# Experts' weights in four DRAM copies, constants of the start moved, and new limits for the planner of a hybrid block

## The chip, the cores and the metric

The kernel runs on one core of a Trainium2 chip, in one launch. Its time is device microseconds, the median of several runs. The core's engines have instruction queues of their own: TensorE (PE; its weight loads are shown apart as PEld), VectorE (DVE), ScalarE (ACT), GpSimd (POOL), and SyncE (SP), on which this kernel issues every DMA.

## The reference

The input x has 8 sequences of 512 rows of 128 numbers, all fp32. Four layers are applied one after another, each on the layernorm of x and each added to x:

```python
x = x + attn_a(layernorm(x))      # state-space layer ("mamba")
x = x + ffn(layernorm(x))         # 8 experts, all of them computed
x = x + attn_b(layernorm(x))      # attention, 16 heads of 8, window of 25 rows back and chunks of 10
x = x + ffn(layernorm(x))         # the same weights again
```

The state-space layer projects x by W_in, runs a convolution of three taps and a SiLU over both halves of the channels, and from one half forms delta, decay, B and C; it then scans over the 512 rows with 8 states in each of 64 channels:

```python
state = decay * state + (1 - decay) * tanh(b) * xb
y = sum(state * tanh(c)) + D * xb
out = concat([y, zb]) @ W_out.T
```

The expert layer weighs all eight experts by the product of two softmaxes:

```python
router_probs = softmax(x @ w_router)
gate_weights = softmax((x @ w_gating) / 0.1)
g = einsum("bsh,ehf->ebsf", x, w_gate)
u = einsum("bsh,ehf->ebsf", x, w_up)
expert_out = einsum("ebsf,efh->ebsh", silu(g) * u, w_down)
cw = router_probs * gate_weights
cw = cw / (sum(cw) + 1e-9)
out = einsum("ebsh,bse->bsh", expert_out, cw)
```

## The kernel before

**The main stream.** Nearly all of TensorE's time goes to the experts' products. `ffn_stream` goes through both expert layers (k = 0, 1), the 8 sequences b, the 8 experts e and four blocks of 128 hidden columns f. For each it issues `g` and `u` (128 hidden columns by 512 rows) and `y` (back to 128 columns, summed over f in one PSUM bank). To keep fp32 precision, every product is three matmuls of split operands: each weight is a rounded part and a rest ("low", `wg`, `wu`, `wd`; the rests are made by the lane `lows` on GpSimd in the beginning), and so are the activations `xt` and `h`. ScalarE takes the SiLU of `g`, VectorE multiplies by `u`, and the hidden block `h` is split into its parts by a cast (ScalarE or VectorE) and a subtraction on GpSimd.

**The experts' weights.** `ffn_prep` computes for a sequence the layernorm, the transposed `xt`, the router's logits, the softmaxes and `cw`. `cw` is transposed (`cps`, copied to `cwt`) and written to DRAM (`cwd`). The lane `spreads` reads it back for each expert as `cwb`, 128 partitions by 512 rows, all partitions alike. VectorE multiplies `y` by `cwb` in place, and GpSimd adds the result to `acc`. There are two buffers for `cwb`.

**The order.** The order of instructions on each engine is not written by hand. While the program is built, a planner issues them one by one: `Engine.__getattr__` issues each instruction (so nearly all of them carry its line, L269, in the profile) and adds its estimated cost to a `Clock` with one time for each engine. Side work is written as generators ("lanes"), which yield the engine that they need next, or a condition. `Lanes.start` says when a lane's next step can begin by these estimates; a step on TensorE is let in between main products only if its operands are there by a margin, `SIDE`, and a larger one where the main stream would first have to be left for it: `JOIN`, or `JOIN_MAX`, `JOIN_ATT`, `JOIN_END` for certain lanes. `HELD` cuts how far ahead of its start a side step may be issued while the main stream waits; `LATE` and `PREP_DUE` set by when the router's exponentials and the preparation of a sequence are due, in sequences. Where the planner sees TensorE waiting, `keep_warm` puts a matmul on constants in (`warm` before the first expert, `idle` after it), if the gap is above `WARM_GAP`. ScalarE has to load a table when it goes from SiLU or tanh to exponentials and back.

**The start.** The first sequence is done in two halves of 256 rows, so that the experts begin early: `first_halves` does its state-space layer (convolution `mv`; `mxb`, `mzb`; `mbc`, `mde`, `macc`; `mbx`, `mcx`, `mdec`; the scan `mst`; the output `mo`) and `ffn_prep` its preparation. The first `SPLIT` experts of the first sequence are then computed for each half by itself, in products of 256 columns; the rest in products of 512. Constants are made meanwhile: `wxz`, the output weights scaled by D, in `mamba_consts` on ScalarE (two instructions, after the flag `done["halves"]`), and `route`, the router's weights with the gating part times 10, in `route_consts` on VectorE (two instructions, L1016 and L1018). The flag `done["quiet"]` holds back the lane `lows` and the second half's inputs while the first half's layernorm runs.

Of the kernel before, what the change touches and what calls it, by code (L numbers as in the profile page):

```python
# [18 lines left out]
P = 128  # L19
# [68 lines left out]

TABLES = {AF.Silu: (18,), AF.Exp: (0, 6), AF.Ln: (6,), AF.Tanh: (0, 18)}
INF = float("inf")  # L90
LAGS = {"T": 0.2, "A": 0.15, "V": 0.15, "P": 0.08}
TO_PE = 0.11
SAME = 0.125
AHEAD = 0.2
EDGE = 0.1
FIRST = 0.6
LATE = 0.3
SIDE = 0.5
JOIN = 2.0
JOIN_DUE = 0.0  # L100
JOIN_MAX = 6.0
JOIN_ATT = 3.0
JOIN_END = 2.0
MOST = 6
OTHERS = 4
AT_FIRST = 7
WARM = 3.5
WARM_GAP = 0.25
WARM_TO = 1.5
SECOND = 0.2  # L110
PRESS = 0.4
HELD = 0.18
MAMBA_DUE = 0.9
PREP_DUE = 0.9
ATT_LEAD = 2.5
EARLY = 5
SPLIT = 4
EARLIEST = 2 * (DEPTH + 1)


# [8 lines left out]
class Clock:  # L129
# [105 lines left out]
    def run(self, key, name, out, args, kw, after, wait):  # L235
        c = self.cost(key, name, out, args, kw)
        start = max(self.end[key] + wait, after, self.now if key == "T" else self.based(key))
        if key == "T":
            if start > self.end["T"] + 2.4:
                self.cold = start  # L240
            if start < self.cold + 3.4:
                c *= 2
        if key in "VP" and self.shares(key, name, out, args):
            start = self.with_port(start, c)
        self.end[key] = start + c
        if key == "S":
            start = max(start, self.now)
            row = out.shape[-1]
            rows = out.shape[0] * size(out) // row
            each = max(row * (2 if out.dtype == BF16 else 4), 512)  # L250
            move = rows * each / 200e3
            self.moved = max(self.moved, start + c + 0.8) + move
            return self.moved + 0.6 + move
        self.hop[key] = start + c
        return start + c + LAGS[key]

# [121 lines left out]
def block_kernel(ctx: ExitStack, tc: tile.TileContext, x, pack_a, pack_b, pack_c, w_qkv, mask, mask_t, w_o,  # L378
# [194 lines left out]
    def mamba_consts(sb, mc):  # L573
        table("natural_log_exp_and_others", 6)

        pick = sb.tile([P, L], F32, tag="dec", name="pick", bufs=5)[:, : 2 * DSTATE]
        pool.tensor_tensor(pick, ident[:, : 2 * DSTATE], ident[:, 32 : 32 + 2 * DSTATE], ALU.add)
        sel = sb.tile([P, 2 * NSTEP, 2, INNER], F32R, name="sel", bufs=1)
        for m in range(2):
            rows = pick[:, m * DSTATE : m * DSTATE + DSTATE].rearrange("p (s i) -> p i s", s=2)  # L580
            pool.tensor_copy(
                sel[:, m * NSTEP : m * NSTEP + NSTEP], rows[:, :, :, None].to_broadcast([P, NSTEP, 2, INNER])
            )
        mc["sel"] = sel.rearrange("p n s c -> p n (s c)")
        yield "A", pa_there

        nega = sb.tile([P, NSTEP], F32, name="nega", bufs=1)
        alog = pa[:, A_ALOG : A_ALOG + NSTEP]
        sp_ = sb.tile([P, NSTEP], F32, tag="sp_a", name="sp_a", bufs=1)
        act.activation(sp_, alog, AF.Abs)  # L590
        act.activation(sp_, sp_, AF.Exp, scale=-1.0)
        act.activation(sp_, sp_, AF.Ln, bias=1.0)
        win = [sb.tile([P, P], F32R, name=f"win_{i}", bufs=1) for i in range(2)]
        src = pa[:, A_WIN : A_WIN + P]
        act.copy(win[0], src)
        yield "V"
        dve.scalar_tensor_tensor(sp_, alog, 0.0, sp_, ALU.max, ALU.add)
        dve.tensor_scalar(nega, sp_, 1e-4, -1.0, ALU.add, ALU.mult)
        dve.tensor_tensor(win[1], src, win[0].bitcast(F32), ALU.subtract)
        mc["win"] = win  # L600
        yield "A"

        cap = sb.tile([P, NSTEP], F32, name="cap", bufs=1)
        act.activation(cap, nega, AF.Exp, scale=1e-4)
        table("silu_and_others", 18)

        yield "T", pc_there
        wp = yield from side([P, P], "wdt_ps")
        pe.matmul(wp, pc[:, 0:P], pc[:, P : 2 * P], start=True, stop=True)
        wdt = sb.tile([P, P], F32, name="wdt", bufs=1)  # L610
        yield "A"
        freed(act.copy(wdt, wp))
        mc["wdt"] = wdt

        wbc = sb.tile([P, P], F32, name="wbc", bufs=1)
        yield "P"
        for h in range(2):
            pool.tensor_copy(
                wbc[INNER * h : INNER * h + INNER].rearrange("p (c n) -> p c n", c=4),
                pa[:INNER, None, A_PBC : A_PBC + 32].to_broadcast([INNER, 4, 32]),  # L620
            )
        mc["wbc"] = wbc
        yield "V"
        dve.tensor_scalar(cap, cap, 1.0, None, ALU.min)
        mc["nega"], mc["cap"] = nega, cap

        yield lambda: "halves" in done
        yield "AV"
        wxz = sb.tile([P, P], F32, name="wxz", bufs=1)
        act.activation(wxz[:INNER], pa[:INNER, A_WOUT : A_WOUT + P], AF.Copy, scale=pa[:INNER, A_D : A_D + 1])  # L630
        mc["wxz"] = wxz, act.copy(wxz[INNER:], pa[INNER:, A_WOUT + P : A_WOUT + 2 * P])
        route_consts()
# [72 lines left out]
    def first_halves(sb, consts, h, xo):  # L705
# [12 lines left out]
        def half(c):  # L718
            cs = slice(c * HALF, c * HALF + HALF)
            v, xb = vs[c], xbs[c]  # L720
            yield "A"
            act.activation(v, h[:, cs], AF.Copy, scale=kc[1])
            yield "V"
            n = 1 - c
            dve.scalar_tensor_tensor(
                v[:, n:], h[:, cs.start + n - 1 : cs.stop - 1], kc[0], v[:, n:], ALU.mult, ALU.add
            )
            yield "V"
            e = dve.scalar_tensor_tensor(
                v[:, : HALF - c], h[:, cs.start + 1 : cs.stop + n], kc[2], v[:, : HALF - c], ALU.mult, ALU.add  # L730
            )
            if c:
                freed(e)
            yield "A"

            act.activation(xb[0:INNER], v[0:INNER], AF.Silu)
            there2 = act.activation(xb[INNER:P], v[0:INNER], AF.Silu)
            yield "T", there2
            pde, pbc = yield from sides(([P, HALF], f"mde0_{c}"), ([P, L], f"mbc0_{c}"))
            pbc = pbc[:, :HALF]  # L740
            pe.matmul(pbc, consts["wbc"][:INNER], xb[:INNER], start=True, stop=True)
            pe.matmul(pde, consts["wdt"][INNER:], xb[INNER:], start=True, stop=True)
            add[c](scanned(c, pbc, pde))

        def scanned(c, pbc, pde):
# [3 lines left out]
            def rows():  # L749
# [3 lines left out]
                act.activation(pbc[32:64], pbc[32:64], AF.Tanh)  # L753
                there["z"] = act.activation(zb, vs[c], AF.Silu)
                issued["tanh"] += 1
                yield "V"
                e = freed(dve.tensor_tensor(bc[32:64], pbc[32:64], bc[32:64].bitcast(F32), ALU.subtract))
                for m, into in enumerate((bxs, ccs)):
# [98 lines left out]
            for p in range(2):  # L857
                yield lambda: p in scans
                yield from undisturbed()
                yield "V", max(scans[p][1], ccs["t", p])  # L860
                cx = sb.tile([P, 2, HALF], F32, tag="acc", name=f"mcx0_{c}_{p}")
                e = freed(dve.tensor_tensor(cx, ccs[p], scans[p][0], ALU.mult))
                yield "T", e
                for t in range(2):
                    for i in range(2):
                        pe.matmul(
                            ops[t], cx[:, i, t * P : (t + 1) * P], pa[:, A_WOUT : A_WOUT + P],
                            start=False, stop=(p == i == 1),
                        )
            yield "V"  # L870
            part = xo[0][:, 2 * c : 2 * c + 2]
            for t in range(2):
# [150 lines left out]
    def ffn_prep(k, b, xc, t0=0, nt=NT):  # L1023
# [13 lines left out]
            done.pop("quiet", None)  # L1037
            done["calm"] = 0.0
        if t0 == 0:
            done["cw", k, b] = dram.tile([NT, NE, P], F32, tag="cwd", name=f"cwd_{nm}", bufs=3), 0.0, 0  # L1040
        cwd = done["cw", k, b][0]
        ready[k, b] = ready[k, b][0], cols.stop
        wr, = routes
# [28 lines left out]


        yield "V"
        cw = fp.tile([P, NT, NE], F32, tag="cw", name=f"cw_{nm}")[:, :nt]
        s4 = fp.tile([P, NT], F32, tag="s4", name=f"s4_{nm}")[:, :nt]
        z = fp.tile([P, NT], F32, tag="z", name=f"z_{nm}")[:, :nt]
        dve.tensor_reduce(s8, pr, AX.X, ALU.add)
# [11 lines left out]
        yield "T"  # L1090
        cps = yield from side([NT * NE, P], f"cps_{nm}")
        n = nt * NE
        pe.transpose(cps[:n], cw.rearrange("p t e -> p (t e)"), ident)
        yield "V"
        cwt = fp.tile([NT * NE, P], F32, tag="cwt", name=f"cwt_{nm}")
        freed(dve.tensor_copy(cwt[:n], cps[:n]))
        yield "S"
        e = sp.dma_start(out=cwd[t0 : t0 + nt].rearrange("t e p -> (t e) p"), in_=cwt[:n])
        done["cw", k, b] = cwd, e, cols.stop

    pos = [0.0]
# [21 lines left out]
    def ffn_stream():  # L1123
# [73 lines left out]
        def spreads():  # L1197

            for k in range(2):
                for b in range(B):  # L1200
                    todo = passes(k, b)
                    for i, (e, cs) in enumerate(todo):
# [6 lines left out]
                        n = cs.stop - cs.start  # L1209
                        cwb = fp.tile([P, L], F32, tag="cwb", name=f"cwb{k}_{b}_{e}_{cs.start}", bufs=2)[:, :n]  # L1210
                        state["cwb", (k, b, e, cs.start)] = cwb, sp.dma_start(
                            out=cwb.rearrange("p (t q) -> p t q", q=P),
                            in_=cwd[None, cs.start // P : cs.stop // P, e, :].to_broadcast([P, n // P, P]),
                        )

        def chunks(cs):
# [644 lines left out]
```

## Time and profile before

| | |
|---|---|
| median of 3 runs | 1353.25 us (1351.0 to 1355.0) |
| the profiled execution | 1351.62 us, span 1349.8 us |
| instructions on record | 29533 |
| DVE, ACT, POOL busy | 1036.8, 964.7 and 940.4 us |
| queue of the DMAs | 33.9% of 16 engines, 105.87 MB |
| `cwb` reads | 124 of 256 KB, 8 of 128 KB |
| mean granted TensorE clock | 0.996 |

The page describes one execution. A row of a group gives the line, the engine, the operation and its tiles (written tile <- read tiles, numbers left out), then counts and times. `PE u <- ACT h` among the waits means that a matmul into `u` waited until an instruction of ScalarE on `h` had ended; the numbers behind are the total in us, the times, and the longest. In a row of windows the numbers are: from and to, the length, the busy time of PE, PEld, DVE, ACT and POOL with instructions in brackets, the granted clock of TensorE as a share of full speed, the DMA engines' busy share and the GB/s moved.

### The profile page before, as it was taken

The numbers are of one execution on the slowest core, as the hardware profiler recorded it, in microseconds if no ns is written. First come the engines' busy times: TensorE is split into PE (matmuls) and PEld (weight loads), VectorE is DVE, ScalarE is ACT, GpSimd is POOL, SyncE is SP. The second block draws the span as 40 slices with busy tenths as digits, with TensorE's granted clock in tenths as the row PEclk, the third lists the DMA queues.
The fourth block names the chain that finished last, engine by engine and source line by source line (L and its number), as shares of the span: only waits on it lengthen the run. The fifth ranks groups of instructions, "written<-read, shape, count | busy, mean of one in ns | idle before, by whom it ended". The sixth has DMA issues, their size and how long they took to land.

```text
span 1349.8 us, 29533 instructions
## 1 busy us (share of the span) xinstructions
PE 1328.9 (98%) x10261; PEld 1053.3 (78%) x10261; DVE 1036.8 (77%) x3114; ACT 964.7 (71%) x1694; POOL 940.4 (70%) x1042
## 2 busy tenths in 40 slices
PE   7999999999999999999999999999999999999998
PEld 7877778788788877777777777777777777778887
DVE  6887888688888867898788887888888787855443
ACT  7768576867787556777777777777877767765654
POOL 5877576776767757666766767767677676777776
PEclk9999999999999999999999999999999999999999
DMA  3321304232112242344345444454544434222111
GB/s 126 95 72 38 87 24 101 62 81 73 45 48 56 63 85 54 73 97 118 79 103 111 99 106 100 104 109 89 118 91 104 119 71 88 61 69 55 40 40 40
DMA packets 230861, 107.75 MB, mean 80 GB/s; under 512 B 86417, under 2 KB 226616, under 8 KB 230712
## 3 DMA queue, kind: packets, MB, share of 16 engines
q1 hardware_dynamic: 230712, 105.87, 33.9%
q8 instruction: 81, 1.33, 0.4%
q14 instruction: 68, 0.56, 0.1%
HBM read 77.64 MB, written 27.79 MB: 78 GB/s over the span
## 4 chain that ended last, share of the span: by engine, by line
PE 89%; POOL 3%; ACT 3%; issue 3%; DVE 2%; DMA 0%; POOLq 0%; DVEq 0%
PE u L269 25%; PE y L269 25%; PE g L269 25%; PE ao L269 2%; PE aw L269 2%; PE as L269 2%; POOL h L269 1%; PE mo L269 1%; PE aqk L269 1%; ACT h L269 1%; DVE h L269 1%; PE mde L269 1%; PE aout L269 1%; PE yp L269 1%; ACT L269 1%
## 5 line engine op out<-in xcount | busy, mean ns | idle before, releaser
L269 POOL TENSOR_TENSOR h<-h,h 128x512 fp32r<-128x512 f32 x492 | 640.0, 1310 | 279.0 <-ACT h L269 219.4
L269 PE MATMUL u<-xt_f,wu 128*128 128x512 f32 (+1 forms) x1584 | 451.5, 395 | 3.5 <-ACT h L269 2.7
L269 PE MATMUL g<-xt_f,wg 128*128 128x512 f32 (+1 forms) x1584 | 448.3, 393 | 2.1 <-ACT h L269 1.9
L269 PE MATMUL y<-h,wd 128*128 128x512 f32 (+1 forms) x1584 | 445.5, 392 | 1.4 <-POOL h L269 0.8
L269 DVE TENSOR_TENSOR h<-u,h 128x512 f32<-128x512 f32 x420 | 285.9, 686 | 157.5 <-PE u L269 109.3
L269 ACT ACTIVATE h<-g 128x512 f32<-128x512 f32 x512 | 303.4, 597 | 123.2 <-PE g L269 100.1
L269 ACT CAST h<-h 128x512 fp32r<-128x512 f32 x437 | 268.4, 619 | 171.2 <-DVE h L269 169.6
L269 PEld LDWEIGHTS g<-xt_f,wg 128*128 128x128 f32 x1584 | 288.5, 189 | 70.3 <-ACT h L269 3.0
L269 PEld LDWEIGHTS y<-h,wd 128*128 128x128 f32 x1584 | 288.3, 188 | 70.2 <-POOL h L269 1.4
L269 PEld LDWEIGHTS u<-xt_f,wu 128*128 128x128 f32 x1584 | 286.6, 189 | 71.7 <-ACT h L269 4.1
L269 POOL TENSOR_TENSOR acc<-acc,cwb 128x512 f32<-128x512 f32 (+1 forms) x114 | 148.0, 1298 | 52.5 <-DVE cwb L269 33.8
L269 ACT ACT_TABLE_LOAD x109 | 139.8, 1283 | 24.7 <-PE g L269 23.2
L269 DVE CUSTOM_DVE_ANT_0 amasked<-as,maskq 128x60 f32<-128x60 f32 x640 | 95.4, 213 | 5.0 <-PE as L269 4.8
L269 DVE TENSOR_TENSOR cwb<-y,cwb 128x512 f32<-128x512 f32 (+1 forms) x116 | 77.5, 668 | 16.0 <-PE y L269 14.4
L269 DVE TENSOR_TENSOR apt<-aw,maskk 125x400 f32<-125x400 f32 (+2 forms) x160 | 88.1, 570 | 0.0
L269 DVE SCALAR_TENSOR_TENSOR h<-h,g 128x512 f32<-128x512 f32 x92 | 62.3, 681 | 27.0 <-ACT h L269 26.6
L269 ACT ACTIVATE apt<-apt 125x400 f32<-125x400 f32 (+2 forms) x160 | 81.5, 540 | 0.4
L269 DVE SCALAR_TENSOR_TENSOR h<-u,h 128x512 f32<-128x512 f32 x92 | 62.6, 683 | 3.3 <-PE g L269 0.5
L269 DVE DVE_READ_ACCUMULATOR2_ANT amx<- 128x1 f32 x640 | 52.1, 81 | 0.0
L269 DVE CAST h<-h 128x512 fp32r<-128x512 f32 x75 | 48.8, 651 | 1.2
L269 DVE COPY v<-avr 125x128 f32<-125x128 f32 (+2 forms) x40 | 25.7, 644 | 26.4 <-PE ao L269 26.4
L269 PEld LDWEIGHTS ao<-apt,v 125*32 125x32 f32 (+2 forms) x1280 | 27.4, 109 | 14.6 <-DVE h L269 4.4
(205 smaller groups left out, 1239.5 us busy)
## 6 DMA issues: line engine op xcount, KB each, us to landing
cwb<-cwd_f SPq DMA_DIRECT2D x124, 256.0 KB
aqd<-apc SPq DMA_DIRECT2D x32, 192.0 KB
ks<-aqd SPq DMA_DIRECT2D x48, 93.8 KB
x_fo<-x SPq DMA_DIRECT2D x16, 256.0 KB
aqd<-apc SPq DMA_DIRECT2D x32, 128.0 KB
x_f<-x SPq DMA_DIRECT2D x15, 256.0 KB
qs<-aqd SPq DMA_DIRECT2D x48, 75.0 KB
aod<-aos SPq DMA_DIRECT2D x24, 100.0 KB
```

The costliest lines, as they stand in the source:

```text
L269: f(*args, **kw)
```

## The change

- `cw` is laid out expert by expert. For a sequence done as a whole, `cwd` holds four copies (`COPIES`), written by one DMA from a repeated source; `cwb` is then read as one contiguous row of 2 KB for each partition, 32 partitions from each copy, and no longer as four pieces of 512 bytes. For the first sequence, done in halves, there is one copy, with pieces of 1 KB.
- In the convolution of the first sequence, the second half's taps on VectorE are planned only after the first half's.
- `wxz` and the `route` constants wait for a new flag, `done["rows"]`, which is set after the first half's tanh and SiLU have been issued.
- `done["quiet"]` is set already after the first half's output products.
- The planner's constants are changed, and its estimate of when a DMA lands.

```diff
@@ -88,33 +88,34 @@
 
 TABLES = {AF.Silu: (18,), AF.Exp: (0, 6), AF.Ln: (6,), AF.Tanh: (0, 18)}
 INF = float("inf")
+COPIES = 4
 LAGS = {"T": 0.2, "A": 0.15, "V": 0.15, "P": 0.08}
 TO_PE = 0.11
 SAME = 0.125
 AHEAD = 0.2
 EDGE = 0.1
 FIRST = 0.6
-LATE = 0.3
-SIDE = 0.5
-JOIN = 2.0
+LATE = 0.4
+SIDE = 0.6
+JOIN = 2.5
 JOIN_DUE = 0.0
-JOIN_MAX = 6.0
-JOIN_ATT = 3.0
-JOIN_END = 2.0
+JOIN_MAX = 10.0
+JOIN_ATT = 5.0
+JOIN_END = 5.0
 MOST = 6
 OTHERS = 4
 AT_FIRST = 7
 WARM = 3.5
-WARM_GAP = 0.25
+WARM_GAP = 0.8
 WARM_TO = 1.5
 SECOND = 0.2
 PRESS = 0.4
-HELD = 0.18
+HELD = 0.1
 MAMBA_DUE = 0.9
-PREP_DUE = 0.9
+PREP_DUE = 0.7
 ATT_LEAD = 2.5
 EARLY = 5
-SPLIT = 4
+SPLIT = 5
 EARLIEST = 2 * (DEPTH + 1)
 
 
@@ -249,8 +250,8 @@
             rows = out.shape[0] * size(out) // row
             each = max(row * (2 if out.dtype == BF16 else 4), 512)
             move = rows * each / 200e3
-            self.moved = max(self.moved, start + c + 0.8) + move
-            return self.moved + 0.6 + move
+            self.moved = max(self.moved, start + c + 0.6) + move
+            return self.moved + 0.8
         self.hop[key] = start + c
         return start + c + LAGS[key]
 
@@ -624,7 +625,7 @@
         dve.tensor_scalar(cap, cap, 1.0, None, ALU.min)
         mc["nega"], mc["cap"] = nega, cap
 
-        yield lambda: "halves" in done
+        yield lambda: "rows" in done
         yield "AV"
         wxz = sb.tile([P, P], F32, name="wxz", bufs=1)
         act.activation(wxz[:INNER], pa[:INNER, A_WOUT : A_WOUT + P], AF.Copy, scale=pa[:INNER, A_D : A_D + 1])
@@ -721,6 +722,9 @@
             yield "A"
             act.activation(v, h[:, cs], AF.Copy, scale=kc[1])
             yield "V"
+            if c:
+                yield lambda: "conv" in issued
+                yield "V"
             n = 1 - c
             dve.scalar_tensor_tensor(
                 v[:, n:], h[:, cs.start + n - 1 : cs.stop - 1], kc[0], v[:, n:], ALU.mult, ALU.add
@@ -731,6 +735,7 @@
             )
             if c:
                 freed(e)
+            issued["conv"] = 1
             yield "A"
 
             act.activation(xb[0:INNER], v[0:INNER], AF.Silu)
@@ -753,6 +758,7 @@
                 act.activation(pbc[32:64], pbc[32:64], AF.Tanh)
                 there["z"] = act.activation(zb, vs[c], AF.Silu)
                 issued["tanh"] += 1
+                done["rows"] = 0.0
                 yield "V"
                 e = freed(dve.tensor_tensor(bc[32:64], pbc[32:64], bc[32:64].bitcast(F32), ALU.subtract))
                 for m, into in enumerate((bxs, ccs)):
@@ -867,6 +873,8 @@
                             ops[t], cx[:, i, t * P : (t + 1) * P], pa[:, A_WOUT : A_WOUT + P],
                             start=False, stop=(p == i == 1),
                         )
+            if c == 0:
+                done["quiet"] = 0.0
             yield "V"
             part = xo[0][:, 2 * c : 2 * c + 2]
             for t in range(2):
@@ -1037,7 +1045,8 @@
             done.pop("quiet", None)
             done["calm"] = 0.0
         if t0 == 0:
-            done["cw", k, b] = dram.tile([NT, NE, P], F32, tag="cwd", name=f"cwd_{nm}", bufs=3), 0.0, 0
+            copies = COPIES if nt == NT else 1
+            done["cw", k, b] = dram.tile([copies, NE, NT, P], F32, tag=f"cwd{copies}", name=f"cwd_{nm}", bufs=3), 0.0, 0
         cwd = done["cw", k, b][0]
         ready[k, b] = ready[k, b][0], cols.stop
         wr, = routes
@@ -1072,7 +1081,8 @@
 
 
         yield "V"
-        cw = fp.tile([P, NT, NE], F32, tag="cw", name=f"cw_{nm}")[:, :nt]
+        cw_rows = fp.tile([P, NE * NT], F32, tag="cw", name=f"cw_{nm}")[:, : NE * nt]
+        cw = cw_rows.rearrange("p (e t) -> p t e", e=NE)
         s4 = fp.tile([P, NT], F32, tag="s4", name=f"s4_{nm}")[:, :nt]
         z = fp.tile([P, NT], F32, tag="z", name=f"z_{nm}")[:, :nt]
         dve.tensor_reduce(s8, pr, AX.X, ALU.add)
@@ -1090,12 +1100,17 @@
         yield "T"
         cps = yield from side([NT * NE, P], f"cps_{nm}")
         n = nt * NE
-        pe.transpose(cps[:n], cw.rearrange("p t e -> p (t e)"), ident)
+        pe.transpose(cps[:n], cw_rows, ident)
         yield "V"
         cwt = fp.tile([NT * NE, P], F32, tag="cwt", name=f"cwt_{nm}")
         freed(dve.tensor_copy(cwt[:n], cps[:n]))
         yield "S"
-        e = sp.dma_start(out=cwd[t0 : t0 + nt].rearrange("t e p -> (t e) p"), in_=cwt[:n])
+        if nt == NT:
+            e = sp.dma_start(
+                out=cwd.rearrange("r e t p -> (e t) r p"), in_=cwt[:, None, :].to_broadcast([n, COPIES, P])
+            )
+        else:
+            e = sp.dma_start(out=cwd[0, :, t0 : t0 + nt, :], in_=cwt[:n])
         done["cw", k, b] = cwd, e, cols.stop
 
     pos = [0.0]
@@ -1209,8 +1224,10 @@
                         n = cs.stop - cs.start
                         cwb = fp.tile([P, L], F32, tag="cwb", name=f"cwb{k}_{b}_{e}_{cs.start}", bufs=2)[:, :n]
                         state["cwb", (k, b, e, cs.start)] = cwb, sp.dma_start(
-                            out=cwb.rearrange("p (t q) -> p t q", q=P),
-                            in_=cwd[None, cs.start // P : cs.stop // P, e, :].to_broadcast([P, n // P, P]),
+                            out=cwb,
+                            in_=cwd[:, None, e, cs.start // P : cs.stop // P, :]
+                            .rearrange("r o t q -> r o (t q)")
+                            .to_broadcast([cwd.shape[0], P // cwd.shape[0], n]),
                         )
 
         def chunks(cs):
```

## The prediction

> **What bounds the kernel now.** I read the page first: busy time and the chain. TensorE is busy for 1328.9 of 1349.8 us and is 89% of the chain; DMA is 0%.
>
> ```profile
> PE 1328.9 (98%) x10261; PEld 1053.3 (78%) x10261; DVE 1036.8 (77%) x3114; ACT 964.7 (71%) x1694; POOL 940.4 (70%) x1042
> PE 89%; POOL 3%; ACT 3%; issue 3%; DVE 2%; DMA 0%; POOLq 0%; DVEq 0%
> ```
>
> So only the 21 us in which PE is idle, slowed or filled can be won. The windows show where (second column: length; third: PE busy; the 1.00 and 0.91 near the end: granted clock):
>
> ```profile
> 20.00:30.00 10.00, 7.43 (x51) 7.22 (x51) 9.28 (x22) 9.33 (x20) 3.63 (x3) 0.83 0.00 0
> 60.00:80.00 20.00, 18.21 (x110) 15.20 (x110) 16.56 (x41) 18.66 (x31) 15.49 (x21) 0.91 0.30 86
> 100.00:200.00 100.00, 96.22 (x438) 74.66 (x438) 77.82 (x164) 73.43 (x125) 68.23 (x73) 0.98 0.20 52
> 400.00:1000.00 600.00, 599.11 (x5701) 469.55 (x5700) 495.82 (x1797) 435.50 (x766) 415.15 (x495) 1.00 0.42 92
> 1300.00:1350.00 50.00, 45.73 (x204) 36.67 (x202) 18.67 (x31) 24.52 (x41) 34.02 (x27) 1.00 0.15 37
> ```
>
> The middle loses 0.9 us in 600. What can move lies before 275 us: the start (first `g` at 34.31 us) and the waits of the early experts. The end loses 4.3 us, but the order of its last instructions is the same in both programs. The waits of PE:
>
> ```profile
> PE u L269 <- ACT h L269: 2.7, 3, 1.4
> PE g L269 <- ACT h L269: 1.9, 1, 1.9
> PE mbc L269 <- ACT mxb L269: 1.8, 1, 1.8
> ```
>
> Three waits for ScalarE's `h` and one for the convolution's SiLU are the largest that the edits can reach.
>
> **Part 1, the start.** The timeline shows what the moved constants cost (start, length):
>
> ```profile
> 9.26 0.53 DVE L1016 COPY route<-pb 128x32 f32<-128x32 f32 x1
> 9.56 0.40 ACT L269 ACTIVATE wxz<-pa 64x128 f32<-64x128 f32 x1
> 9.71 1.30 POOL L269 TENSOR_TENSOR wu<-stageu,wu 128x512 fp32r<-128x512 f32 x1
> 9.83 1.21 DVE L1018 TENSOR_SCALAR route<-route 128x8 f32<-128x8 f32 x1
> 9.97 0.30 ACT L269 COPY wxz<-pa 64x128 f32<-64x128 f32 x1
> 10.30 0.48 ACT L269 ACTIVATE mv<-mh,pa 128x256 f32<-128x256 f32 x1
> ```
>
> `wxz` holds ScalarE until 10.27, while `mh` ends at 9.91: moving it lets the first scaling start 0.2 to 0.5 us sooner. The tap order on VectorE is the same in both programs, so "half 0 first" moves nothing. The route scale, 8 columns, took 1.21 us and ended at 11.04, 0.03 after GpSimd's `wu`. In the new order copy and scale stand after `macc` of half 0 (14.13) and before the subtraction of `mbc` (14.69). There GpSimd runs `wu` from 14.06 to 15.34, so the subtraction waits until about 15.4 and `mbx`, half 1's tanh and the table load behind them come some 0.5 us later. Against that, the second `mbx` multiply (27.74, 0.69 us) moves behind the layernorm statistics on VectorE, which was busy for 9.28 of these 10 us. GpSimd's weight lows stand before `va_f` in both orders (nine of them), so "GpSimd kept free" changes no order. Sum for the first `g`: −0.3 + 0.5 − 0.6 = −0.4, rounded to −0.3 as the residual adds then wait for `mo`; range −0.7 to +0.8.
>
> **Part 2, the fillers.** WARM_GAP 0.8 takes the idle matmuls after the start from 30 to 7. Products waited for idle matmuls in six places:
>
> ```profile
>   PEld u L269: 0.8, 3
>   PEld g L269: 0.5, 2
>   PEld y L269: 0.3, 1
> ```
>
> That is 1.6 us; by their pitch (11 warm matmuls from 9.74 on, 0.12 us each) 23 of them are 2.8 us. Nothing is gained where a filler stood in a real wait. I take −2.2, range 0 to −2.8. Ten warm matmuls fewer lie in the start's waits: 0.
>
> **Part 3, the clock.** Two windows after the start ran at half clock, each behind one in which PE idled:
>
> ```profile
> 67.40:70.83 3.43, 2.28 (x9) 1.18 (x8) 3.38 (x11) 3.38 (x5) 0.97 (x2) 1.00 0.01 3
> 70.83:74.25 3.42, 3.42 (x15) 3.03 (x15) 2.51 (x8) 3.41 (x8) 2.65 (x5) 0.50 0.26 76
> 173.20:176.65 3.45, 1.51 (x8) 0.90 (x6) 1.29 (x3) 3.42 (x6) 2.35 (x2) 1.00 0.14 36
> 176.65:180.06 3.41, 3.41 (x8) 2.74 (x9) 2.42 (x4) 2.11 (x4) 1.82 (x2) 0.50 0.17 40
> ```
>
> In 176.65–180.06 PE got through 8 products of 512 columns, at 0.233 us each 1.87 us of work: 1.5 us lost. Busy time of 2.27 was enough to bring a half window once, while 1.83 (9.4–12.8 us) and 2.02 (262.0–265.4 us) did not, so the threshold is not sharp. Fewer fillers speak for more such windows, the moved side work for fewer. I take one of two gone: −1.5, range −3.0 to +1.5.
>
> The Trainium skill, page "TensorE: Matmul & The Clock Gate", Part 1, has the clock fall only after a whole idle window of about 3.4 us. Here it fell after windows with 1.5 and 2.3 us of work, so the rows decide; by the page the fillers could go at no risk and this term would be 0 to −3.0.
>
> **Part 4, the replanned order.** SPLIT 5 gives 72 products of 256 columns for 36 of 512: six narrow ones take 0.72 us where three wide ones take 0.70, +0.24 in all. PE leaves the main products for side work 211 times instead of 210, so JOIN and SIDE bundle nothing. In the new order the exponentials and side groups that stood before `h` at 173.8 (wait 1.94) and 260.8 (1.4) stand elsewhere; a table load, four exponentials and a load back (1.28 us a load) now stand between two SiLUs of an expert near 1020 us, where PE would wait up to 2.4. Net −1.0, range −3.3 to +3.8. Twelve casts of `h` go from VectorE (651 ns) to ScalarE (619 ns) and table loads rise by two; both engines have a quarter free. Nothing.
>
> **Part 5, four copies.** `cwb` is read as 128 pieces of 2 KB, not 512 of 512 B. By packet records of 84–108 and 27–35 ns this is 0.67–0.86 us on 16 engines, was 0.86–1.1. The trace says who waits for it:
>
> ```profile
>   DMA cwb<-cwd_f: 0.5, 2
> ```
>
> From issue to its reader there are 11.7 us in the median of 132, 2.9 at least, under 5.75 in ten: the faster read gains nothing. The write of `cwd` grows from 16 to 64 KB, 0.2 us more, 15 times, ahead of the first `cwb` of a sequence, inside the same slack. Issuing costs SP more: other three-level patterns took 0.57–0.61 us (`aat_t`, `ks`), `cwb` 0.39. SP is not on the chain. Term 0, bounded by the third rival.
>
> Sum: −0.3 − 2.2 − 1.5 + 0.24 − 1.0 = −4.8 us. The profiled execution took 1351.62 (span 1349.8 and 1.8 around it), so it would take 1346.8; the median of the runs, 1353.25, lies 1.6 higher: 1348.4.
>
> **Rivals.** (a) *Nothing that matters*: fillers stood in real waits (five of them lie in the 2.1 us before 70.52, where `u` waits for `h`), the half windows recur at other places, the waits only move. Then −0.3 + 0.24 + 0 to −2: about 1352. For it: side groups are as many as before. Against: six waits directly on idle matmuls.
>
> (b) *The order gets worse at the late expert*: 2.4 us of waiting plus one half window of 1.5, fillers in real waits: −0.3 + 0.24 + 3.9 = +3.8, 1357; only with both windows kept. It ends on the slow edge of no change.
>
> (c) *Slower by late `cwb`*: the new read names four copies outermost, a form with no row in the trace. Bounds: 128 pieces sixteen at a time 0.67 us, one at a time 10.8–13.8. VectorE takes its queue in order: a late `cwb` holds its multiply, the next `h` products and a PSUM bank, and then PE. Below 2.9 us nothing is late; if two to three pieces move at a time and it lands 5.75 us after issue, ten transfers are late by up to 2.9, about 1 us each: +10 − 4.8 = +5, 1358. Landings seen so far (isolated reads: 2.1–3.4 us from first to last packet) speak against it.
>
> The Trainium skill, "DMA: Bandwidth & Descriptors", section on why a DMA increments its semaphore by 16, speaks against this edit: a DMA uses the largest number of engines up to 16 that divides the outermost counts of both patterns, here 4. By that, 32 pieces on each engine are an estimated 2.7–3.4 us, which the slack still hides: 0 to +1. No run here shows it yet.
>
> **How the numbers follow.** A difference of 0.3% (4.06 us) is about what this measurement can tell from none. Forecast 0.52, (a) 0.29 with the good half of (b), (c) and the rest of (b) 0.19. Low end: each term at its best, −0.7 − 2.8 − 3.0 + 0.24 − 3.3 = −9.6, and 2.25 for the runs' spread: 1341.4. High end: (c), 1358. The forecast's own range is 1341.4 to 1349.
>
> **What would show it.** First `g` at 33.5–34.5; `wxz` gone from before `mv`; the route scale beside GpSimd's `wu`; 7 idle matmuls and no wait on them; at most one half window between 40 and 300 us; `cwb` still under 1 us among the waits. It is wrong if PE waits rise after 300 us, if DVE's waits for `cwb` exceed 5 us, or if half windows stay at two or more.

## The result, and the profile after

The changed kernel is slower: 1368.07 us in the median of 6 runs (1365.26 to 1374.68) against 1353.03 (1351.0 to 1355.01), a ratio of 1.0116 with a 95% interval of 1.0091 to 1.0142. That is +15 us; the forecast was −4.8. The profiled execution has a span of 1372.9 us, and is the longest of the six runs, so its stage figures add up to 6.6 us more than the median.

Busy time and chain of the changed kernel, the lines that answer to the first two of the prediction:

```profile
PE 1333.4 (97%) x10264; PEld 1055.6 (77%) x10264; DVE 1029.9 (75%) x3090; ACT 965.2 (70%) x1714; POOL 940.1 (68%) x1044
PE 78%; DMA 6%; ACT 6%; DVE 4%; issue 3%; POOL 2%; SPq 1%; POOLq 0%; DVEq 0%; ACTq 0%
```

PE does nearly the same work, but its share of the chain fell from 89% to 78%, and DMA went from 0 to 6%. The windows of the changed kernel (from:to, length, PE busy, …, granted clock):

```profile
20.00:30.00 10.00, 6.79 (x44) 6.38 (x43) 8.21 (x14) 8.84 (x21) 2.48 (x2) 0.84 0.01 2
60.00:80.00 20.00, 16.62 (x120) 14.63 (x119) 18.52 (x44) 19.78 (x38) 17.32 (x23) 0.95 0.21 66
100.00:200.00 100.00, 96.56 (x455) 75.16 (x454) 76.62 (x158) 75.05 (x131) 67.27 (x69) 1.00 0.21 61
400.00:1000.00 600.00, 591.17 (x5575) 460.38 (x5573) 475.15 (x1742) 433.05 (x768) 399.70 (x476) 0.99 0.36 90
1000.00:1200.00 200.00, 193.83 (x1934) 150.18 (x1927) 156.93 (x573) 140.98 (x259) 137.40 (x164) 0.99 0.34 87
```

PE's busy time from 60 to 80 us fell (16.62, was 18.21), but that is no loss, because these windows count the idle matmuls as work. Alone they have in that stretch, first before, then after:

```profile
60.00:80.00 20.00, 3.34 (x9) 1.68 (x9) 0.91 0.30 86
60.00:80.00 20.00, 0.39 (x1) 0.19 (x1) 0.95 0.21 66
```

With idle and warm matmuls counted as idle time, PE stands still for 36.9 us up to 400 us, before for 37.0, and both kernels have three half-clock windows there. Counted by the columns of `g` and `u` in both traces, the changed kernel is 3.4 us behind in the first products, level (0.1 us or less) at those which before reaches at 371 and 435 us, and 23.3 us behind at that of 1232 us. So nearly all is lost where the prediction saw nothing to win or lose: from 400 to 1000 us PE now idles for 8.8 us (was 0.9), and for 6.2 from 1000 to 1200. These are the stretches of the attention. Its loads and stores go over the DMA queue, and the waits name them (waiter, what it waited for, us in all, times, longest):

```profile
DVE cwb L270 <- DMA cwb<-cwd_f: 10.1, 6, 4.8
DVE st_a L270 <- DMA x_a<-x: 10.0, 7, 2.3
...
DVE aover L270 <- DMA aover<-aod: 9.7, 6, 3.6
...
DVE aat_t L270 <- DMA aall_over<-aoverd: 6.8, 3, 3.8
```

Before, the first three of these rows read 0.5, 0.6 and 1.3 us, and the fourth was not there. All waits of compute engines and weight loads for DMAs come to 75 us, against 14. One of them, in order of time (start, length, engine):

```profile
813.08 0.61 SPq L270 DMA_DIRECT2D cwb<-cwd_f  x1
...
813.78 0.59 SPq L270 DMA_DIRECT2D aall_over<-aoverd  x1
...
821.01 0.69 DVE L270 TENSOR_TENSOR aat_t<-aat_t,aall_over 128x512 f32<-128x512 f32 x1 [3.76 <-DMA aall_over<-aoverd]
821.62 1.28 DVE L270 TENSOR_TENSOR h<-u,h 128x512 f32<-128x512 f32 x2
...
822.36 1.65 PE L270 MATMUL u<-xt_f,wu 128*128 128x512 f32 x3 [2.42 <-DVE h L270]
```

In the trace VectorE works through its instructions in order. The attention's multiply stands ahead of the expert's, so the expert's `h` waits for a load that has nothing to do with it, and PE waits for `h`. The three matmuls behind the wait then need 1.65 us, as a half-clock window follows (822.1 to 825.5). The changed kernel has five such windows after the first `g`, three of them after 400 us; before there were two, none of them after 400 us.

The load itself was late. It was issued 0.1 us behind a `cwb` read and landed 6.5 us after its issue; the seven other loads of `aall_over` took 2.4 to 3.5. So it is with `aover` (16 KB): 12 of its 16 loads now go out while a `cwb` read is under way and take 3.5 us in the median, the other four 1.5. Before, 3 of the 16 went out so.

### The profile page after: what moved, and what is told of

Same layout as the page of the kernel before. It is cut to its first block, busy times and chain, and to the rows that moved or that the text cites. A ratio compares the mean times of both kernels' runs of the same rounds, so it can differ in the third digit from the quotient of the medians.

```text
span 1372.9 us, 29464 instructions
## 1 busy us (share of the span) xinstructions
PE 1333.4 (97%) x10264; PEld 1055.6 (77%) x10264; DVE 1029.9 (75%) x3090; ACT 965.2 (70%) x1714; POOL 940.1 (68%) x1044
## 4 chain that ended last, share of the span: by engine, by line
PE 78%; DMA 6%; ACT 6%; DVE 4%; issue 3%; POOL 2%; SPq 1%; POOLq 0%; DVEq 0%; ACTq 0%
PE u L270 22%; PE y L270 22%; PE g L270 21%; PE ao L270 2%; ACT h L270 2%; DMA x_a<-x 2%; PE aw L270 2%; PE mo L270 1%; PE as L270 1%; DVE h L270 1%; ACT L270 1%; SPq L270 1%; POOL h L270 1%; DMA aover<-aod 1%; DMA aqd<-apc 1%
## 5 line engine op out<-in xcount | busy, mean ns | idle before, releaser
L270 DVE TENSOR_TENSOR h<-u,h 128x512 f32<-128x512 f32 x426 | 288.8, 685 | 163.2 <-PE u L270 94.6
L270 PEld LDWEIGHTS y<-h,wd 128*128 128x128 f32 x1596 | 291.7, 190 | 73.2 <-POOL h L270 2.8
L270 DVE SCALAR_TENSOR_TENSOR h<-h,g 128x512 f32<-128x512 f32 x86 | 58.5, 682 | 26.2 <-ACT h L270 25.6
L270 DVE SCALAR_TENSOR_TENSOR h<-u,h 128x512 f32<-128x512 f32 x86 | 58.5, 684 | 3.5 <-DVE s_f L270 0.2
L270 DVE CAST h<-h 128x512 fp32r<-128x512 f32 x73 | 45.0, 621 | 1.2
```

Of the source, the lines that this page charges most:

```text
L270: f(*args, **kw)
```

## The experiments

Several kernels below have exactly the instruction order of another one and differ in one transfer. The trace's DMA landing events show, for each transfer, how many engines reported and when.

**1. The landing estimate, undone and alone.** Besides the constants, the change shortens the planner's estimate of when a DMA lands: for 256 KB from 4.0 us after the issue (0.8 + 0.6 and twice 1.31) to 2.7 (0.6 + 0.8 and once 1.31). The trace of before has 4.83 in the median for `cwb`.

```diff
 # e1: the changed kernel with this undone; e2: the kernel before with this done
-            self.moved = max(self.moved, start + c + 0.8) + move
-            return self.moved + 0.6 + move
+            self.moved = max(self.moved, start + c + 0.6) + move
+            return self.moved + 0.8
```

> The changed kernel with one thing undone: the planner's estimate of when a DMA lands (lead 0.8 us, landing after the move 0.6 us, the move counted twice, as before). Theory 1 (the new estimate is too early, so steps that need a DMA are ordered too soon and stall their engine's queue): most of the 15 us come back, 1351 to 1358 us; waits of VectorE and ScalarE for DMAs, some 54 us in the seven largest rows of the changed kernel, fall under 10. Theory 2 (the read from four copies runs on four DMA engines and delays all transfers): 1363 to 1370, waits stay. Theory 3 (the planner's other limits or the start): 1360 to 1370, but the DMA waits fall.

> The kernel before with one thing done: the new landing estimate. Theory 1: 1360 to 1370 us, with waits of VectorE for cwb, x_a, aover and aall_over as in the changed kernel. Theories 2 and 3: 1350 to 1357.

Undone: 1369.91 us, nothing came back, though waits for DMAs fell from 75 to 39 us, as theory 3 forecast. Alone: 1368.77 us, a ratio of 1.0125 (1.0106 to 1.0144), with 60 us of waits for DMAs. So the estimate alone is enough for the whole loss, and yet undoing it brings nothing back. Theory 1 holds for one of the two and not for the other.

**2. The copies, in an unchanged order, and the number of engines.**

```diff
 # e3: before, with cw expert by expert, four copies and this read
+                            .rearrange("r o t q -> r o (t q)")
+                            .to_broadcast([cwd.shape[0], P // cwd.shape[0], n]),
 # e4: the changed kernel, e5: e3, each with this read in its place
+                            .rearrange("r o t q -> o r (t q)")
+                            .to_broadcast([P // cwd.shape[0], cwd.shape[0], n]),
```

> The kernel before with one thing done: four copies of cwd and the reads from them. The order of instructions on every engine is that of before, instruction for instruction, so only the transfers differ. Theory 1: 1351 to 1356 us, waits of VectorE for cwb under 3 us. Theory 2: 1358 to 1368, cwb landing late and other transfers behind it.

> The changed kernel with the read of cwb written so that its outermost count is 32 (partition groups) and the copies lie inside: same bytes, pieces and order of instructions on every engine. It should give 16 landings for each read, where the changed kernel shows 4. Theory 2: 1353 to 1360 us. Theory 1: 1364 to 1370, with waits for cwb a little smaller (10.1 us to 5 or so) and the others as they are.

> The kernel before with the four copies alone, but read with the outermost count of 32, so on 16 engines; the order of instructions on every engine is that of before. If the transfers of before were hidden (as the prediction had it), 1352 to 1355 us, like the copies on 4 engines (1354.3). If the medium-late landings of before still cost something, 1348 to 1351. cwb should land about 3.2 us after its issue in the median, as in the changed kernel on 16 engines, where before has 4.8.

| read of `cwb` | landings for each | us to landing, median (9 in 10) | in before's order | in the change's order |
|---|---|---|---|---|
| 512 x 512 B, one copy | 16 | 4.83 (5.67) | 1353.0 | 1366.21 (e13) |
| 128 x 2 KB, four copies outermost | 4 | 4.84 (6.29) | 1354.28 (e3) | 1368.07 |
| 128 x 2 KB, four copies inside | 16 | 3.23 (3.93) | 1351.45 (e5) | 1358.20 (e4) |

The landing figures are of the kernels before, after and e4, counted from the end of SP's instruction to the last landing. The Trainium skill, "DMA: Bandwidth & Descriptors", in its section on the semaphore's 16, says that the outermost counts of a DMA's patterns set how many engines it runs on, and this is confirmed: with an outermost count of four the read posts 4 landings, with 32 it posts 16. So the change made the pieces four times as large and gave them a quarter of the engines, and the read came no sooner. With 16 engines it comes 1.6 us sooner, and in the changed order that is worth 9.9 us, as theory 2 forecast. Other loads gain too: the twelve of `aover` behind a `cwb` read, 3.5 us in the changed kernel, take 1.7 in e4, with no change of order. The waits of e4:

```profile
DVE st_a L270 <- DMA x_a<-x: 6.9, 6, 2.2
...
DVE cwb L270 <- DMA cwb<-cwd_f: 3.4, 3, 1.8
...
DVE aover L270 <- DMA aover<-aod: 2.3, 2, 1.2
```

and PE's windows in the same run: the stretch of 800 to 1200 us, where the changed kernel has 390.66 busy, got 6.5 of its 9.3 idle microseconds back, and 40 to 100 us is as it was (54.96 there):

```profile
40.00:100.00 60.00, 54.91 (x401) 51.01 (x402) 53.54 (x112) 42.74 (x81) 47.26 (x55) 0.94 0.27 76
800.00:1200.00 400.00, 397.14 (x4025) 309.06 (x4024) 325.85 (x1207) 301.07 (x537) 271.74 (x325) 1.00 0.40 94
```

In before's order the same step, from e3 (ratio 1.0008, 0.9997 to 1.0019) to e5 (0.999, 0.998 to 1.000), is worth some 2.4 us: there e3 came out as theory 1 had it, and e5 just between its two forecasts. How much a read costs depends on the order that it stands in.

**3. The old read and a single copy, in the change's order.**

```diff
 # e13: four copies written, one read as before (its old layout of cw is left out here)
-                            out=cwb,
+                            out=cwb.rearrange("p (t q) -> p t q", q=P),
+                            in_=cwd[0, None, cs.start // P : cs.stop // P, e, :].to_broadcast([P, n // P, P]),
 # e14: rows of 2 KB, all from the first copy
-                            in_=cwd[:, None, e, cs.start // P : cs.stop // P, :]
-                            .to_broadcast([cwd.shape[0], P // cwd.shape[0], n]),
+                            in_=cwd[:1, None, e, cs.start // P : cs.stop // P, :]
+                            .to_broadcast([1, P, n]),
```

> The changed kernel, order of instructions unchanged on every engine, with the read of before (512 pieces of 512 bytes on 16 engines, one copy read; four are still written). If the four engines are what costs in this order: 1357 to 1361 us, like the 2 KB read on 16 engines (1358.2). If the new order needs the faster read, and any read that lands after 4.8 us costs: 1364 to 1370.

> The changed kernel, order unchanged, with all 128 partitions reading rows of 2 KB from the first copy alone (outermost count 128, 16 engines). If the copies do nothing and the engines everything: 1357 to 1360 us and landings near 3.2 us, as with four copies on 16 engines. If reading one copy from 16 engines at once is slow: over 1361.

The old read gives 1366.21 us. Its runs (1363.9 to 1368.8) overlap with those of the four engines (1365.3 to 1374.7), so in this order it is not clearly better. So the four engines are not what made the kernel slower than before; they are why the copies brought nothing. One copy in rows of 2 KB gives 1358.23 us and 3.20 us to landing, the same as four. What helps is the contiguous row on 16 engines; the copies do nothing that shows.

**4. The start and the limits, each alone, and a single copy in their orders.**

```diff
 # e6: before with the edits of first_halves and "rows" in mamba_consts alone
+                yield lambda: "conv" in issued
+                done["rows"] = 0.0
+                done["quiet"] = 0.0
 # e7: before with the ten limits from LATE to SPLIT alone
 # e17, e18: e6 and e7 with cw expert by expert, read as rows
+COPIES = 1
```

> The kernel before with the edits of the start alone (taps, flag rows for the constants, quiet). Theory A (route at GpSimd's port delays the first expert, 1.2 us in the changed kernel's profile): 1354 to 1357 us, first g at 35 to 36 us. Theory B (the start costs nothing that lasts): 1352 to 1354.

> The kernel before with the planner's ten limits alone (LATE to SPLIT), old landing estimate and old read. The prediction's parts 2 to 4: 1348 to 1351 us, 7 or so idle matmuls. If they are what remains of the loss on 16 engines (5 us): 1356 to 1360.

> The order of the sixth experiment (edits of the start alone, 1366.9 us), instruction for instruction, with cw laid out expert by expert in one copy and read as rows of 2 KB on 16 engines. If orders other than that of before lose by late transfers: 1355 to 1360 us, VectorE's waits for cwb (9.3 us there) gone. If this order is bad for other reasons: 1363 to 1367.

> The order of the seventh experiment (the planner's ten limits alone, 1367.7 us), instruction for instruction, with one copy read as rows of 2 KB on 16 engines. Late transfers: 1355 to 1361 us. Other reasons: 1363 to 1368.

The start alone: 1366.91 us. The limits alone: 1367.65. Both lie outside all that was expected of them. Each part costs about what the whole change costs, so the parts do not add up, which speaks for the new order that each brings and not for fifteen microseconds of this or that edit. The faster read, in the same orders, takes back 3.4 (1363.47) and 4.7 us (1362.97); the waits for DMAs go from 39 to 14 and from 34 to 18 us, near before's 14, and three quarters of the loss stay. Most of the added standstill lies before 400 us: idle and warm matmuls left out, PE stands still up to there for 42.7 us in e17 and 41.9 in e18 (37.0 in before), and from 400 to 1200 for 2.5 and 3.6 (1.3). e17 also has three half-clock windows more.

**5. Orders that mean nothing.** Two limits of the kernel before moved by a hundredth and by a tenth:

```diff
 # e9
-MAMBA_DUE = 0.9
+MAMBA_DUE = 0.91
 # e10
-JOIN_MAX = 6.0
+JOIN_MAX = 6.1
```

> The kernel before with a limit that the change does not touch moved by a hundredth (MAMBA_DUE 0.90 to 0.91). The order is that of before up to the 720th of 12653 instructions on TensorE's queue, and another from there on. Theory 4 (what costs is not any one edit: the order of before is a lucky one among many, and any other order that these estimates give meets late transfers): 1360 to 1370 us. Theory 5 (the edits themselves are bad): 1351 to 1355.

> The kernel before with JOIN_MAX 6.0 to 6.1, which changes the order only from the 4732nd of 12653 instructions on TensorE's queue, in the attention. Theory 4: the attention's share of the loss, 5 to 12 us: 1358 to 1365 us, with VectorE's waits for DMAs up. Theory 5: 1351 to 1355.

e9 took 1348.57 us, a ratio of 0.9961 (0.9948 to 0.9974), e10 1358.87, 1.0040 (1.0025 to 1.0055). Theory 4 expected both to be slower and was wrong on the first; theory 5 was wrong on both. What stands is the size: a limit moved by a hundredth moves the time by −5 us, and another one, moved by a tenth, by +5. e9 wins in one place. It is level with before up to the product that before reaches at 125 us, and 4.2 us ahead at that of 183: PE idles for 1.1 us there and not for 2.8 (length less the third column), and the half-clock window is gone. The stretch in e9, then in before:

```profile
140.00:200.00 60.00, 58.90 (x275) 46.36 (x274) 45.94 (x98) 43.43 (x77) 39.93 (x44) 1.00 0.22 58
140.00:200.00 60.00, 57.16 (x260) 44.76 (x259) 47.51 (x99) 40.23 (x66) 39.42 (x41) 0.97 0.22 58
```

**6. Later estimates, and the change without its start.**

```diff
 # e11: the changed kernel
-            self.moved = max(self.moved, start + c + 0.6) + move
-            return self.moved + 0.8
+            self.moved = max(self.moved, start + c + 0.8) + move
+            return self.moved + 1.4 + move
 # e8: e1 with the read on 16 engines; e12: e4 without the edits of the start
```

> The changed kernel with a landing estimate 0.8 us later than the one of before (lead 0.8, landing 1.4 after a move counted twice, so 4.8 us for a cwb; the measured median is 4.8). If late transfers are what costs, whatever the edits: waits for DMAs fall from 75 us to under 20 and the time to 1354 to 1361 us, even on four engines. If the order is bad for other reasons: 1365 to 1371.

> The changed kernel with the old landing estimate and the read on 16 engines: the order of instructions is that of the first experiment (1369.9 us) on every engine, only the read of cwb differs. If that one's loss too is the four engines' (10.8 us of waiting for cwb there): 1352 to 1359 us. If its order is bad for another reason: 1363 to 1370.

> The changed kernel on 16 engines without the edits of the start (taps, rows, quiet). The changed kernel on 16 engines took 1358.2 us, of which some 5 us more than before are lost before 100 us. If the start's edits are the cause: 1352 to 1355 us, first g at 34.3. If not: 1356 to 1360.

With the estimate set to the measured 4.8 us, e11 is the slowest of all, 1381.55 us, though its waits for DMAs fell to 30 us, not to under 20. A truer estimate did not give a better order, which speaks against theory 1 as a rule. e8 against e1 is another pair of one order with two reads: 1356.98 against 1369.91, 12.9 us for the 16 engines. e12 went the other way from the expectation, 1367.67 us where e4 has 1358.20: taking the start's edits out of the change made it slower. The 5 us that the expectation saw lost before 100 us are nearly all idle and warm matmuls that are not there: without them, PE stands still up to there for 31.3 us in e4 and 30.8 in before, with one half-clock window more in e4.

**7. The idle matmuls, and the fastest version.** In e16 the planner still counts them, but they are not issued; all other instructions keep their order. e15 is e9's order with the four copies on 16 engines.

```diff
 # e16
-                freed(pe.matmul(t[:, :HALF], sel[:, 0], sel[:, : HALF // P], start=True, stop=True), "experts")
+                a = t[:, :HALF], sel[:, 0], sel[:, : HALF // P]
+                freed(clock.run("T", "matmul", a[0], a, dict(start=True, stop=True), 0.0, 0.0), "experts")
```

> The kernel before without its 30 idle matmuls, which are planned but not issued; all other instructions are in the same order. The prediction's second step: 1350 to 1353 us (0 to 2.8 gained). If the idle matmuls keep the clock up: 1354 to 1358, with more than three half-clock windows.

> The order of the ninth experiment (1348.6 us; MAMBA_DUE 0.91) with the four copies read on 16 engines; the order is the same instruction for instruction. In the order of before the faster read brought 1.2 us, in that of the change 10: here 1346 to 1348 us, and the fastest version of this study.

e16: 1352.32 us against 1352.56, a ratio of 1.000 (0.9991 to 1.0008). Its profile shows four half-clock windows' length between 57 and 82 us, where before has one (third column: PE busy; the 0.89: granted clock):

```profile
40.00:100.00 60.00, 53.93 (x346) 47.57 (x345) 48.52 (x104) 44.36 (x79) 46.60 (x54) 0.89 0.26 75
```

e15: 1349.25 us, 0.9978 (0.9969 to 0.9987) of before. It beats both kernels, but the gain over e9 that was expected did not come: the two ratios' intervals overlap. In both, PE idles for 0.3 us from 400 to 1200 us, which leaves a faster read nothing to win there.

## Why the prediction was wrong

**The step that failed is Part 4**, the replanned order: "Net −1.0, range −3.3 to +3.8", taken from waits that could be followed by hand before 300 us and one near 1020. With Parts 1 to 3 the new order was to bring −4.8 us. In that order with the read of before it is +13.7 (e13, against 1352.56), of which a faster read takes back 8. Seven other orders, run with the read of before or on four engines, gave −5 to +28. A range of a few microseconds was far too narrow for an order whose matmuls differ from the 14th on.

**A term was not taken that belongs there.** The diff's new landing estimate stood in the text about the kernel, but no term was worked out for it; alone it costs 15.6 us (e2), though undoing it alone brings nothing back (e1). The prediction priced each transfer against the slack that the trace of before showed, "11.7 us in the median of 132, 2.9 at least", and wrote "SP is not on the chain". That slack is a property of one order, and the same change replaced the order. DMA's 0% of the chain became 6%, and 14 us of waits 75. Part 5's 0 for the read itself was about right: on four engines it differs from the old read by 1.1 us in before's order (e3) and by 1.9 in the change's (e13), neither clear of noise.

**Rival (c)** had the right side and waiter, VectorE's waits for `cwb`, but not the mechanism. In the median the reads landed no later (4.84 us, was 4.83), though one in ten took over 6.3 (was 5.7); and with the read of before in the new order (e13) the waits for `cwb` are still 9.0 us. What changed is the few tightest readers: the shortest time from the issue to VectorE's being free for the product fell from 2.9 to 0.9 us, while the median hardly moved (11.5 and 11.2). And `cwb` was 10 us of 75; `x_a`, `aover` and `aall_over`, which the change does not touch, were more; of these, 12 loads of `aover` and one of `aall_over` now go out behind a `cwb` read and land late. The page's rule on outermost counts was right, and so was the estimate's size, 2.7 to 3.4 us of moving: from a read's first packet to its last it took 3.3 in the median. Part 5's own times from packet records were too short: the old read took 3.4 by that measure, not 0.86 to 1.1, and rows of 2 KB on 16 engines 2.0 (e4), not 0.67 to 0.86. But "the slack still hides" it was again before's slack.

**Part 1** said first `g` 0.3 us sooner; it came at 35.54, 1.23 later. The route copy and scale did end up ahead of the subtraction, as said:

```profile
14.72 0.85 DVE L1024 COPY route<-pb 128x32 f32<-128x32 f32 x1
15.61 0.17 DVE L1026 TENSOR_SCALAR route<-route 128x8 f32<-128x8 f32 x1
15.81 0.42 DVE L270 TENSOR_TENSOR mbc<-mbc,mbc 32x256 fp32r<-32x256 f32 x1
```

The subtraction at 15.81 was forecast for 15.4. The copy ended as GpSimd's `wu` did (15.57 and 15.54), and the scale, with GpSimd idle, took 0.17 us where it had taken 1.21. But `mh` ended at 10.60 (9.91 before), so the first scaling came 0.33 us later and not sooner. In both programs eight warm matmuls stand ahead of `mh`; before they took 1.19 us, here 2.05:

```profile
7.75 1.19 PE L269 MATMUL warm<-sel 128*128 128x256 f32 x8
7.84 2.05 PE L270 MATMUL warm<-sel 128*128 128x256 f32 x8
```

They start 0.12 us apart before and 0.21 here, where the record of a full clock begins at 9.76 us (5.98 before). That belongs to the execution and not to the order: e14 has the same order, a full clock from 5.89 us on, the end of `mh` at 9.71, the first scaling 0.55 us sooner than before, and its first `g` at 34.19. It is no clean test either, as before lost a half-clock window ahead of the first `g` and e14 none. With before's order up to there, the first `g` came at 34.31, 34.38 (e5), 36.52 (e10) and 37.15 (e3). One profile of each kernel cannot tell 0.3 us from nothing, so Part 1 stays undecided.

**Part 2** (−2.2) is 0.0 ± 1.2 (e16). The 1.6 us of weight loads that waited for idle matmuls were real. In e16's profile the half-clock windows of 57 to 82 us put it 2.0 us behind, at the product that before reaches at 100 us; it is level again at that of 183, as before's window at 176.65 is missing there. **Part 3** counted on one window less. From 40 to 300 us there are two, as before, and three more stand in the attention, where no term looked; each of these follows a window with 1.2 to 1.9 us of work. It had said that fewer fillers speak for more such windows, and took one of two as gone all the same.

**What stays open**: what the new orders still lose with the fast read. In e4 PE stands still, idle and warm matmuls left out, for 37.1 us up to 400 us, as in before, and for 4.4 us from 400 to 1200 (1.3 in before), with one half-clock window more; that is most of its 5 to 6 us, and its waits for DMAs are still 38 us. e8, with 14 us of such waits, is 4.6 us slower than before all the same (ratio 1.0034). In e12, e17 and e18 the larger part of the added standstill lies before 400 us. No run here takes either apart.

## What to carry to other kernels

When a change touches a planner's estimates, the old trace's slack no longer bounds anything: price the new order as a draw with the spread of other orders, and measure that spread with two or three changes that mean nothing before crediting any edit. To learn what a transfer or a filler is worth, change it alone in an order that is held fixed, and do it in more than one order: the read in rows of 2 KB on 16 engines was worth nothing to 8 us against the old read, and 2.4 to 13 against four engines. Compare stages with the fillers taken out, and take more than one profile where a start of a few tenths is in question. For a broadcast read from DRAM like this one, make the row contiguous and keep a large count outermost; copies were not needed.

## What the runs showed of the hardware

- A 256 KB read that repeats one row over 128 partitions lands 4.83 us after the end of its issue as 512 pieces of 512 bytes on 16 engines, 4.84 as 128 pieces of 2 KB on four, and 3.2 as 128 pieces of 2 KB on 16, from one copy or from four (before, after, e4, e14).
- A small load issued while such a read is under way lands later: `aover`, 16 KB, took 1.5 us alone and 3.5 behind a read on four engines (after), 3.1 behind the old read (e13), and 1.7 behind the fast one (e4).
- Issuing the read took SP 0.39 us (median) before, 0.57 where the source names the copies as a level of their own, and 0.51 from one copy (before, after, e14).
- The clock fell to half behind windows in which TensorE still worked (2.28 of 3.43 us and 1.51 of 3.45 in before): 57 to 82 us in e16 had about 13 us of half clock; before, with idle matmuls, had one window of 3.4 us there.
- In executions of one order the eight warm matmuls ahead of `mh` came 0.12 us apart (e14) or 0.21 (after), and the first `g` at 34.19 or 35.54 us.
